# Graph network layer 0: the attention encoder as one run of steps, its exponentials traced two steps ahead across the parts, and the emptying of the PSUM banks queued behind them

## Chip, cores, metric

The kernel runs on one core of a Trainium2 chip. The metric is the device time of one launch in microseconds (us), the median of several launches. A profile is one further launch recorded by the hardware profiler. Engines are called by the names of the profile: PE is TensorE (matmul), PEld its weight load, DVE is VectorE, ACT is ScalarE, POOL is GpSimd, SP is SyncE, which here only issues DMAs.

## What is computed

Four graph layers follow each other on 2708 nodes with 512 features. Each is `x = layernorm(x + layer(x, adj))`. The change touches only the first attention of layer 0 (the "encoder"). The reference, cut to that part:

```python
n = X.shape[0]                                    # 2708 nodes, 512 features, H = 4 heads of D = 128
Xh = X.reshape(n, H, D).transpose(1, 0, 2)
Xw = jnp.einsum('hnd,hde->hne', Xh, W)
f1 = jnp.einsum('hnd,hd->hn', Xw, V[:, 0, :, 0])
f2 = jnp.einsum('hnd,hd->hn', Xw, V[:, 1, :, 0])
sig = jax.nn.sigmoid(f1[:, :, None] + f2[:, None, :])
...                                               # both patterns are adj, so local_att == long_att
att = softmax over the entries with adj != 0 of adj * sig
Xa = jnp.einsum('hij,hjd->hid', att, Xw)
Xc = Xa.transpose(1, 0, 2).reshape(n, F)
Xn = _batchnorm(Xc, enc_bn_gamma, enc_bn_beta)
emb = _mlp_block(Xn, enc_mlp_W, enc_mlp_b, enc_mlp_bn_gamma, enc_mlp_bn_beta)
...                                               # decoder: att applied to emb, then an MLP block
x = _layernorm(x + out)                           # layers 1 to 3 follow
```

## The kernel before

The softmax weights are never held as a whole. The target nodes (`i`) are split into two halves of 1354 (`hf`, `HSPAN`), the four heads into two pairs (`p`, `HP` = 2), and the source nodes (`j`) into `NT` = 22 blocks of up to 128. One of the four combinations (`hf`, `p`) is here called a **part**: (0,0), (0,1), (1,0), (1,1), in this order. A part walks over the 22 blocks in the order `ORDER`; a block of a part is a **step**, and its number in the part is `place`. So the encoder has 88 steps. `attention_pass` is called with `first=True` for the encoder, and again with `first=False` for the decoder.

`form` makes the weights of one step: a block of 128 sources by 1354 targets for two heads, in a tile `t` of 128 x 2708 floats. It loads a block `a` of the transposed adjacency (L378), and then

- in the parts with `p == 0` (`prepare`): turns zeros of `a` into a large negative number with two DVE instructions (`z` L394, `a` L395) and stores the block to DRAM as `adj_d` on the POOL queue (L399); parts with `p == 1` load that `adj_d` instead;
- two ACT instructions (L406): tanh of f1 + f2, one for each head, the tile `f1b` holding f1 spread over the partitions;
- one DVE instruction (L414) that adds a constant to tanh and multiplies by `a`;
- one ACT instruction (L415): the exponential, of both heads at once.

Some steps (`KEPT`) store `t` to DRAM as well (`kept`, L501, POOL queue), for the decoder. The wide tile `t` comes from a set of five buffers (`wide_tile`), the tile `a` from four, `f1b` from three.

`node_sums(k, ...)` (L436) then multiplies: for head `k` of the pair, 11 matmuls with 128 targets of `t` as weights and the 129 columns of `xw` (128 features and a column of ones for the sum of weights) as the moving operand. Both heads of a step are 2 x 22 records in the profile's count, 44 in all. All eight PSUM banks hold the sums of a part, four for each head, from its first step to its last.

At the end of a part `keep` is called (its result is named `turns`). It traces the **emptying** of the banks: for each head five groups, each of three DVE instructions (L643 clamp of the sum, L644 reciprocal, L645 multiplication into the tile `rows`, which also is one of the five wide tiles). It returns two functions `turn(0)` and `turn(1)`: each transposes the rows of one head on PE (L662, L670) into banks of head 1, copies them to `ft` on DVE (L672, L682), and leaves `bn_stats` (L684) in the list `later`. The loop of the next part calls them: at `place` 0 it traces head 0's sums and `turn(0)`, at `place` 1 head 0's sums and `turn(1)`; head 1's sums of these two steps wait in the list `waiting` until then, since the transposes use head 1's banks.

The order of work: the program traces instructions in the order of the Python code, and a planner at compile time orders each engine's queue by its own model of durations, the order of tracing being the priority; it also hands out the buffers and inserts the waits. Each engine runs its queue in that order. `tc.issue_after(ins)` adds an edge that puts the traced instructions of the same engine behind `ins`. In the kernel before, a dictionary `taken` holds the last L645 of each head; the `form` of `place` 2 of the next part is traced under `issue_after` of these, so that it comes behind the emptying.

Of the kernel before, what the change touches and what calls it, by code (L numbers as in the profile page):

```python
# [8 lines left out]
F32 = mybir.dt.float32  # L9
# [8 lines left out]
P = 128  # L18
# [11 lines left out]
def gnn_stack_kernel(  # L30
# [25 lines left out]
    nc = tc.nc  # L56
    N, F = x.shape
    H = w0.shape[1]
    C = F // P
    NT = (N + P - 1) // P  # L60
# [123 lines left out]
    with ExitStack() as l0:  # L184
# [143 lines left out]
        def spread_sums(att, hf, p):  # L328

            h0, w = HSPAN[hf]  # L330
            t = att.tile([P, HP, HW], F32, tag="rb", name="rb", bufs=1)
            for k in range(HP):
                nc.sync.dma_start(
                    t[:, k, :w], rs_d[HP * p + k, h0 : h0 + w].partition_broadcast(P)
                )
            return t
# [4 lines left out]
        def attention_pass(values, first, att, psum, finish, f1b=None, blocks=(), spread=None, rest=None, taken={}):  # L341
# [84 lines left out]
            def node_sums(k, place, jt, t, w, hf):  # L426

                n = BLOCKS[jt][1]
                slots = list(range(NB))
                if n < P:  # L430
                    slots.sort(key=lambda r: r % PER)
                for r in slots:
                    b, s = divmod(r, PER)
                    i0, m = NODES[hf][r]
                    own = 0 if n == P else b % HB * Q
                    nc.tensor.matmul(  # L436
                        po[k][b][:m, s * DR : (s + 1) * DR],
                        t[own : own + n, k, i0 : i0 + m],
                        values[own : own + n, jt, HP * pair + k, :],
                        start=(place == 0 and s == 0),  # L440
                        stop=(place == NT - 1),
                        skip_group_check=True,
                    )

            later = []
# [3 lines left out]
            turns = []  # L449
            for hf, (h0, w) in enumerate(HSPAN):  # L450
                for p in range(H // HP):
                    prepare = first and p == 0
                    if f1b is None or not prepare or hf > 0:
# [19 lines left out]
                    rb = None if first else spread_sums(att, hf, p)  # L473
                    pair = p
                    waiting = []
                    for place, jt in enumerate(ORDER):
                        n = BLOCKS[jt][1]


                        if place > (3 if first else 0) and later:  # L480
                            later.pop(0)()
                        if first:
                            t = wide_tile(att, "t")[:, : HP * HW].rearrange(
                                "p (k w) -> p k w", k=HP
                            )
                        else:
                            t = att.tile([P, HP, HW], F32, tag="t", name="t", bufs=4)
                        tv = t[:n, :, :w]
                        kept = kept_d.get((hf, p, jt))
                        if kept is None or first:  # L490
                            rows = n if n == P else HR
                            with ExitStack() as order:

                                for ins in taken.values() if place == 2 else ():
                                    order.enter_context(tc.issue_after(ins.ins))
                                step = form(hf, p, jt, att, prepare, f1b, t[:rows, :, :w])
                            if rest is not None:
                                rest(step)
                                rest = None
                            if kept is not None:  # L500
                                nc.gpsimd.dma_start(kept[:n, :, :w], tv)  # L501
                        else:
                            for r in range(0, P if n == P else HB * Q, P if n == P else Q):
                                nc.sync.dma_start(t[r : r + n, :, :w], kept[:n, :, :w])
                            if p == 0 and jt in KEPT[1]:
                                count(hf, jt, att)
                        if po is None:


                            both = [  # L510
                                psum.tile([P, HP, BANK], F32, tag=f"po{q}", name="po", bufs=1)
                                for q in range(HB)
                            ]
                            po = [both[q][:, k, :] for k in range(HP) for q in range(HB)]
                            if first:
                                more = [
                                    psum.tile([P, BANK], F32, tag=f"psm{k}", name="po", bufs=1)
                                    for k in range(HP)
                                ]
                                po = [  # L520
                                    [both[q][:, k, :] for q in range(HB)] + [more[k]]
                                    for k in range(HP)
                                ]
                        if first:
                            node_sums(0, place, jt, t, w, hf)
                            waiting.append(lambda a=(1, place, jt, t, w, hf): node_sums(*a))
                            if turns:
                                turns.pop(0)()
                            if not turns:
                                for work in waiting:  # L530
                                    work()
                                waiting = []
                            continue
                        for k in range(HP):
                            h = HP * p + k
                            for q, (q0, qw) in enumerate(HCH[hf]):
                                r = 0 if n == P else q * Q
                                nc.tensor.matmul(  # L538
                                    po[HB * k + q][:, :qw],
                                    values[r : r + n, jt, h * P : (h + 1) * P],  # L540
                                    t[r : r + n, k, q0 : q0 + qw],
                                    start=(place == 0),
                                    stop=(place == NT - 1),
                                )
                    if first:
                        turns = finish(hf, p, po, later)
                    else:
                        later += finish(hf, p, po, rb) or []
# [65 lines left out]
        with (  # L614
# [5 lines left out]
            taken = {}  # L620
            ft = feat_tile("ft")

            def keep(hf, p, po, later):
# [5 lines left out]
                for k in range(HP):  # L629
# [8 lines left out]
                    for b, g in groups:  # L638
# [6 lines left out]
                        taken[k] = nc.vector.tensor_tensor(  # L645
# [45 lines left out]
            attention_pass(xw, True, att, psum, keep, f1b, blocks, spread, rest, taken)  # L691
# [1378 lines left out]
```

## Time and profile before

| | us |
|---|---|
| median of 3 runs (lowest to highest) | 3199.09 (3196.76 to 3205.66) |
| the profiled execution: its own time | 3197.97 |
| the profiled execution: span from the first to the last instruction | 3196.2 |
| PE busy over the span | 3104.5 (97%) |
| DVE busy | 2050.9 (64%) |
| ACT busy | 1349.7 (42%) |
| encoder: first and last L436 matmul, about | 38.6 to 534.2 |

The mean granted TensorE clock is 0.989. A line of the timeline reads: start in us from the span's start, duration in us, engine, line of the kernel, operation, output and inputs with shapes, count, and in brackets the idle time of that engine just before, with what ended it. Runs of like instructions close together are merged in one line. A line of the windows view gives busy time and count for each engine in a stretch, then the granted clock, the share of DMA time and the transfer rate. A line of a group gives count, busy time and mean ns of one, and the idle time before it. A line of the waits view gives the total, the number and the longest of a kind of wait.

### The profile page before, as it was taken

Reading aid. Unit: us, or ns where it says so; the run is one execution under the profiler, and the core shown is the slowest. Engines: PE = TensorE matmul, PEld = TensorE weight load, DVE = VectorE, ACT = ScalarE, POOL = GpSimd, SP = SyncE. Lnnn points to the kernel's source line nnn. Section 1 sums busy time; section 2 is a strip of 40 time slices with the busy share of each in tenths; the row PEclk is TensorE's granted clock in tenths of the full one; section 3 lists DMA queues with packets and bytes.
Section 4 is the critical chain, followed back from the end, with each engine's and each line's share of the span. In section 5 each row is a group of like instructions: output and inputs, shape, how many; then the busy total and the mean of one; then the engine's idle time right before and its main releaser. Section 6 shows DMA issues by size and latency. Waiting matters only on the chain.

```text
span 3196.2 us, 39584 instructions
## 1 busy us (share of the span) xinstructions
PE 3104.5 (97%) x15176; PEld 2353.4 (74%) x15176; DVE 2050.9 (64%) x3797; ACT 1349.7 (42%) x1615; POOL 204.0 (6%) x304
## 2 busy tenths in 40 slices
PE   8998899999999999999999999999999999999999
PEld 7988887444444446885578787777668888888886
DVE  7878975777686684444167667767644555555565
ACT  7898887477867552001133333434301111111111
POOL 1100100000000000000011111110110000000000
PEclk9999999999999999999999999999999999999999
DMA  7866865146545413541144444556431111111111
GB/s 277 305 216 218 283 244 181 68 153 232 178 159 207 171 62 95 144 127 44 40 149 139 139 143 148 156 172 177 134 101 36 50 52 49 49 51 51 49 44 34
DMA packets 203635, 425.81 MB, mean 133 GB/s; under 512 B 20798, under 2 KB 134562, under 8 KB 197622
## 3 DMA queue, kind: packets, MB, share of 16 engines
q1 hardware_dynamic: 179454, 319.92, 32.3%
q0 software_dynamic: 23552, 101.26, 8.5%
q8 instruction: 119, 1.95, 0.2%
q10 hardware_dynamic: 440, 2.10, 0.2%
q14 instruction: 70, 0.57, 0.1%
HBM read 325.88 MB, written 95.87 MB: 132 GB/s over the span
## 4 chain that ended last, share of the span: by engine, by line
PE 76%; DVE 8%; issue 6%; ACT 5%; DMA 4%; POOL 1%; SPq 0%; DVEq 0%; POOLq 0%; ACTq 0%
PE po L1546 18%; PE ps_s L1342 17%; PE po L538 10%; PE ps_nb L1156 7%; PE po L436 6%; PE ps_wide L1206 5%; PE ps_sup L1734 2%; PE ps_mlp L792 2%; PE ps_hid L131 2%; ACT t L415 2%; ACT t L406 2%; PE ps_dec L923 2%; DVE t L414 2%; PE ps_v L131 1%; DVE e L1832 1%
## 5 line engine op out<-in xcount | busy, mean ns | idle before, releaser
L414 DVE SCALAR_TENSOR_TENSOR t<-t,a 128x2708 f32<-128x2708 f32 (+1 forms) x152 | 450.6, 2975 | 171.0 <-ACT t L406 165.4
L436 PE MATMUL po<-xw,t 128*128 128x129 f32 (+2 forms) x3872 | 444.2, 281 | 43.7 <-ACT t L415 42.6
L436 PEld LDWEIGHTS po<-xw,t 128*128 128x128 f32 (+2 forms) x3872 | 435.4, 192 | 52.0 <-ACT t L415 48.0
L406 ACT ACTIVATE t<-f1b,f2h 128x1354 f32<-128x1354 f32 (+1 forms) x304 | 414.3, 1412 | 55.0 <-PE po L538 33.2
L415 ACT ACTIVATE t<-t 128x2708 f32<-128x2708 f32 (+1 forms) x152 | 371.7, 2453 | 96.7 <-DVE t L414 96.3
L1342 PE MATMUL ps_s<-q,hT 128*128 128x256 f32 (+1 forms) x1848 | 405.5, 372 | 0.0
L538 PE MATMUL po<-t,emb 128*128 128x452 f32 (+3 forms) x1056 | 397.7, 545 | 3.9 <-ACT t L415 3.7
L1546 PE MATMUL po<-sup,e 128*128 128x256 f32 (+1 forms) x1512 | 397.0, 384 | 2.8 <-DVE c L1627 2.1
L1342 PEld LDWEIGHTS ps_s<-q,hT 128*128 128x128 f32 x1848 | 339.2, 190 | 49.8 <-issue 6.8
L538 PEld LDWEIGHTS po<-t,emb 128*128 128x128 f32 (+1 forms) x1056 | 193.6, 190 | 201.1 <-issue 190.6
L1546 PEld LDWEIGHTS po<-sup,e 128*128 128x128 f32 (+1 forms) x1512 | 264.3, 185 | 58.8 <-issue 21.5
L1546 PE MATMUL po<-held,T 128*128 128x256 f32 x1200 | 294.5, 380 | 4.5 <-DVE T L1503 4.5
L1546 PEld LDWEIGHTS po<-held,T 128*128 128x128 f32 x1200 | 226.4, 190 | 38.2 <-DVE T L1503 6.9
L1922 DVE SCALAR_TENSOR_TENSOR e<-a_cols,ps_s 128x512 f32<-128x512 f32 (+1 forms) x121 | 79.7, 659 | 239.4 <-PE ps_s L1342 233.3
L1342 PE MATMUL ps_s<-hT 128*128 128x256 f32 (+2 forms) x968 | 215.6, 374 | 4.1 <-DVE e L1832 2.5
L1342 PEld LDWEIGHTS ps_s<-hT 128*128 128x128 f32 x968 | 175.4, 191 | 31.9 <-DVE e L1832 2.9
L1828 ACT ACTIVATE a_score<-a_score,neg_big 128x512 f32<-128x512 f32 (+2 forms) x131 | 88.7, 686 | 250.1 <-DMA a_score<-in_adj_dram 102.8
L1156 PE MATMUL ps_nb<-hid_hi,at 128*128 128x512 f32 x484 | 185.5, 390 | 0.4 <-DVE at L1148 0.4
L1156 PE MATMUL ps_nb<-hid_lo,at 128*128 128x512 f32 x462 | 179.9, 389 | 0.0
L1452 ACT ACTIVATE e<-e 128x512 f32<-128x512 f32 (+1 forms) x187 | 113.5, 617 | 133.5 <-DVE e L1451 133.1
L1503 DVE TENSOR_TENSOR T<-e 128x256 f32<-128x256 f32 x200 | 83.9, 420 | 124.9 <-PE po L1546 99.2
L1914 ACT ACTIVATE q<-ps_wide,uq 128x256 f32<-128x256 f32 (+1 forms) x44 | 20.5, 465 | 338.4 <-PE ps_wide L1206 338.4
(275 smaller groups left out, 3938.6 us busy)
## 6 DMA issues: line engine op xcount, KB each, us to landing
a<-adj_d SPq DMA_DIRECT2D x108, 677.0 KB
a_cols<-in_adjT_dram SPq DMA_DIRECT2D x200, 256.0 KB
a<-in_adjT_dram SPq DMA_DIRECT2D x42, 677.0 KB
adj_d<-a POOLq DMA_DIRECT2D x42, 677.0 KB, 6.0
kept<-t POOLq DMA_DIRECT2D x20, 1354.0 KB, 7.6
t<-kept SPq DMA_DIRECT2D x20, 1354.0 KB
raw<-in_adjT_dram SPq DMA_DIRECT2D x105, 256.0 KB
a_score<-in_adjT_dram SPq DMA_DIRECT2D x55, 256.0 KB
```

Source lines behind the costliest of these rows:

```text
L131: nc.tensor.matmul(ps[:n], xt[:, c, :n], w[:, c, :], start=(c == 0), stop=(c == C - 1))
L406: tanh = nc.scalar.activation(tv[:, k, :], f1b[k][:n, :w], AF.Tanh, bias=f2h[:n, jt, h : h + 1], scale=0.5,)
L414: step = nc.vector.scalar_tensor_tensor(tv, tv, GUARD, ab, ALU.add, ALU.mult)
L415: exp = nc.scalar.activation(tv, tv, AF.Exp, scale=0.5)
L436: nc.tensor.matmul(po[k][b][:m, s * DR : (s + 1) * DR], t[own : own + n, k, i0 : i0 + m], values[own : own + n, jt, HP * pair + k, :], sta ...
L538: nc.tensor.matmul(po[HB * k + q][:, :qw], values[r : r + n, jt, h * P : (h + 1) * P], t[r : r + n, k, q0 : q0 + qw], start=(place == 0), ...
L1156: nc.tensor.matmul(pos[it][:n], at, half[:, jt, :], start=(jt == 0 and k == 0), stop=(jt == NT - 1),)
L1206: nc.tensor.matmul(ps[:, :width], w(c, o), xt(c), start=(c == 0), stop=(c == C - 1),)
L1342: nc.tensor.matmul(ps[:, jb, i:w], keys[:, c, j : j + P], st["q"][:, c, i:], start=(c == 0), stop=(c == C - 1),)
L1452: nc.scalar.activation(e, e, AF.Exp)
L1546: nc.tensor.matmul(po[bank][rows, half, :], lhsT, rhs, start=(k == 0 and half == 0) if first is None else first, stop=last, skip_group_che ...
L1828: nc.scalar.activation(a, a, AF.Identity, bias=neg_big[: a.shape[0]], scale=1.0e30)
```

## The change

The nested loops over halves, pairs and blocks become one loop over a list `steps` of 88 (for the encoder) with an index `k`. In the encoder, `front` = 2: iteration `k` traces the `form` of step `k`, and then the sums (`node_sums`) of step `k - 2`, whose tile waits in the list `held`. So when the last sums of a part are traced, the first two steps of the next part have been formed already; their `f1b` loads are traced two steps earlier as well. The emptying (`finish`, which is `keep`) is traced under `issue_after(last_step)`, `last_step` being the L414 of the latest formed step, and each `turn` likewise. `taken` and its edges are gone. `later` is looked at beside the sums rather than before `form`. The sums of the decoder move into `feature_sums`, with `front` = 0; the order in which the decoder is traced stays. In `keep` nothing else changes. The core of the diff:

```diff
-        def attention_pass(values, first, att, psum, finish, f1b=None, blocks=(), spread=None, rest=None, taken={}):
+        def attention_pass(values, first, att, psum, finish, f1b=None, blocks=(), spread=None, rest=None):
...
-            def node_sums(k, place, jt, t, w, hf):
+            def node_sums(k, part, place, t):
+                hf, p = part
+                jt = ORDER[place]
...
-            turns = []
-            for hf, (h0, w) in enumerate(HSPAN):
-                for p in range(H // HP):
+            turns, waiting, held = [], [], []
+            parts = [(hf, p) for hf in range(NHALF) for p in range(H // HP)]
+            steps = [(part, place) for part in parts for place in range(NT)]
+            front = 2 if first else 0
+            last_step, rb = None, None
+            for k in range(len(steps) + front):
+                if k < len(steps):
+                    (hf, p), place = steps[k]
+                    h0, w = HSPAN[hf]
+                    jt = ORDER[place]
+                    n = BLOCKS[jt][1]
                     prepare = first and p == 0
-                    if f1b is None or not prepare or hf > 0:
+                    if place == 0 and (f1b is None or k > 0):
...
-                            with ExitStack() as order:
-                                for ins in taken.values() if place == 2 else ():
-                                    order.enter_context(tc.issue_after(ins.ins))
-                                step = form(hf, p, jt, att, prepare, f1b, t[:rows, :, :w])
+                        last_step = form(hf, p, jt, att, prepare, f1b, t[:rows, :, :w])
+                        if rest is not None:
+                            rest(last_step)
+                            rest = None
+                        if kept is not None:
+                            nc.gpsimd.dma_start(kept[:n, :, :w], tv)
...
-                        if first:
-                            node_sums(0, place, jt, t, w, hf)
-                            waiting.append(lambda a=(1, place, jt, t, w, hf): node_sums(*a))
-                            if turns:
-                                turns.pop(0)()
-                            if not turns:
-                                for work in waiting:
-                                    work()
-                                waiting = []
-                            continue
...
-                    if first:
-                        turns = finish(hf, p, po, later)
+                    held.append(t)
+                if k < front:
+                    continue
+                part, place = steps[k - front]
+                t = held.pop(0)
+                if po is None:
+                    po = banks()
+                if not first:
+                    feature_sums(part, place, t)
+                    if place == NT - 1:
+                        later += finish(*part, po, rb) or []
+                    continue
+                if place > 3 and later:
+                    later.pop(0)()
+                node_sums(0, part, place, t)
+                waiting.append(lambda a=(1, part, place, t): node_sums(*a))
+                if turns:
+                    with tc.issue_after(last_step.ins):
+                        turns.pop(0)()
+                if not turns:
+                    for work in waiting:
+                        work()
+                    waiting = []
+                if place == NT - 1:
+                    with tc.issue_after(last_step.ins):
+                        turns = finish(*part, po, later)
...
             def keep(hf, p, po, later):
-                        taken[k] = nc.vector.tensor_tensor(
+                        nc.vector.tensor_tensor(
```

## Prediction

> **What bounds the kernel now.** I read the page first: PE is busy 97% of the span, so only time in which PE stands or runs slowly can be won. The change touches the encoder alone, so next the windows view, cut at the three crossings from one part to the next.
>
> ```profile
> core 0: us, PE busy (x) PEld busy (x) DVE busy (x) ACT busy (x) POOL busy (x), PEclk, DMA share, GB/s
> 38.00:155.00 117.00, 106.73 (x916) 103.63 (x909) 111.30 (x68) 102.33 (x61) 17.62 (x31) 0.96 0.81 283
> 155.00:183.00 28.00, 20.41 (x156) 20.01 (x156) 21.90 (x44) 20.84 (x14) 2.01 (x4) 0.82 0.58 194
> 183.00:275.00 92.00, 91.40 (x839) 90.77 (x838) 59.68 (x29) 90.27 (x55) 5.34 (x11) 1.00 0.68 233
> 275.00:301.00 26.00, 18.08 (x138) 17.61 (x137) 20.85 (x44) 17.84 (x12) 2.12 (x3) 0.80 0.55 206
> 408.00:434.00 26.00, 18.37 (x139) 17.84 (x138) 19.96 (x40) 20.38 (x13) 1.55 (x3) 0.80 0.64 225
> ```
>
> Part (0,0), the row from 38 to 155, is bound by DVE (111.3 of 117 us); part (1,0) alike. Part (0,1), 183 to 275, has PE and ACT full together and DVE at 60. At each crossing nobody is full, and the granted clock falls to 0.8. In the last part 918 matmuls of L436 took 101.05 us on the chain, 0.110 us each; at that price the 433 PE records of the three crossings need 47.7 us, and the crossings last 80. So 32 us is the ceiling of what the change can win.
>
> Then the timeline of the first crossing:
>
> ```profile
> 149.79 2.98 DVE L414 SCALAR_TENSOR_TENSOR t<-t,a 128x2708 f32<-128x2708 f32 x1
> 152.81 2.46 ACT L415 ACTIVATE t<-t 128x2708 f32<-128x2708 f32 x1 [3.03 <-DVE t L414]
> 155.18 7.98 ACT L406 ACTIVATE t<-f1b,f2h 128x1354 f32<-128x1354 f32 x6
> 159.49 0.16 DVE L643 TENSOR_SCALAR rc<-po 128x1 f32<-128x1 f32 x1 [6.72 <-PE po L436]
> 163.99 2.97 DVE L414 SCALAR_TENSOR_TENSOR t<-t,a 128x2708 f32<-128x2708 f32 x1
> 166.99 2.46 ACT L415 ACTIVATE t<-t 128x2708 f32<-128x2708 f32 x1 [3.83 <-DVE t L414]
> 169.50 5.10 PE L436 MATMUL po<-xw,t 128*128 128x129 f32 x22 [7.59 <-ACT t L415]
> 176.33 2.69 PE L436 MATMUL po<-xw,t 128*128 128x129 f32 x22
> 180.78 1.27 DVE L682 COPY ft<-po 128x512 f32<-128x512 f32 x2
> ```
>
> DVE finishes the part's last block at 152.8, idles 6.72 us for the last sums, and empties most of the banks; only then, at 163.99, does it multiply the next part's first block. Its exponential ends at 169.4, and PE, done at 161.9, waits 7.59 us, though head 0's banks were empty long before. Then its 22 matmuls take 5.10 us instead of 2.69. The second crossing:
>
> ```profile
> 260.76 0.87 DVE L394 TENSOR_SCALAR z<-a 128x1354 f32<-128x1354 f32 x1 [4.82 <-DMA a<-in_adjT_dram]
> 274.18 5.35 ACT L406 ACTIVATE t<-f1b,f2h 128x1354 f32<-128x1354 f32 x4
> 279.64 0.16 DVE L643 TENSOR_SCALAR rc<-po 128x1 f32<-128x1 f32 x1 [5.48 <-PE po L436]
> 289.65 5.10 PE L436 MATMUL po<-xw,t 128*128 128x129 f32 x22 [7.59 <-ACT t L415]
> ```
>
> The waits view of the encoder gives both waits in total:
>
> ```profile
> PE po L436 <- ACT t L415: 42.6, 20, 7.6
> DVE rc L643 <- PE po L436: 23.5, 4, 6.7
> ```
>
> **The change part by part.** No arithmetic is added or removed. What moves is the order of three queues around three crossings. Call the next part's steps n0, n1, n2, n3.
>
> *Crossings one and three (from p = 0 to p = 1).* In p = 0 ACT's tanh already runs two steps ahead of its exponentials (the part's last tanh is at 141.87, the last exponential at 152.81), so I expect n0's and n1's tanh in ACT's gaps before 157. Three things must be there. `f1b` was issued at 139.65; the first one of the kernel, issued at 22.9, held its tanh until 30.5, so 7.6 us, 147.3. The block `a`: SP issued at 141.5 and later, landing 5.2 to 11.5 us after, 153 at worst for n0. A wide tile: that of the step five earlier, done on PE at 142. Then on DVE n0 runs 152.8 to 155.8 and n1 to 158.8 (2 x 2.98), inside the 6.72 us of idling: cost nothing, covered by that idle time; without it, 5.95 us of delay of the emptying. The emptying starts at 159.5 as before and, without the multiplications between, lasts 6.2 us (4.6 from 159.49 to 164.1, and 1.6 for the pieces that stood behind L414), until 165.7; head 0's half is done by 162.6. PE: n0 of head 0 162.6 to 165.0 (22 x 0.11); transposes of `turn(0)` once head 1's banks are empty, 165.7 to 167.2; n1 to 169.7; transposes of `turn(1)` to 171.1.
>
> Now the new edges. The copies of each `turn` go behind L414 of n2 and n3: n2 165.7 to 168.7, copies 2.0 us to 170.7, n3 to 173.7, copies to 175.7. What is queued behind them: head 1's sums of n0 wait for banks that `turn(1)` uses. Before, these copies ended at 182.5 (rows 180.78 to 182.46), with n3 already ahead of them, so the edge adds nothing to that order. Head 1 starts at 175.5 instead of 182.5, with the same work behind it on PE: 7.0 us. If n1's tanh stays behind the exponential at 152.81, n1's L414 ends at 160.9 and everything is 1.4 later: 5.6 us. I take 7.0, by the steady order. Part (0,1) must keep the gain: it is full on ACT, 9.95 us for two steps in the timeline (4 tanh, 2 exponentials), and ACT's exponential of n3 moves from 181.6 to about 173.8, 7.8 us, so ACT does not eat it.
>
> *Crossing two (from p = 1 to p = 0).* Here DVE bounds what follows, so its finish counts. Before, both L414 and the emptying are done at 291.3. ACT is full; it makes n0's and n1's tanh at 274.18. If they stay there, n0's L414 ends at 279.8, n1's at 282.8, the emptying at 289.0: 2.3 us. With n0's tanh one exponential earlier (PE has three steps in hand at 267, so the displaced exponential is not late) L414 ends at 277.2 and 281.3, the emptying at 287.5: 3.8. Ceiling 5.5, the whole idle time. I take 3.5.
>
> *What else moves.* SP's loads of `f1b` and `a` and POOL's stores keep their order among themselves; `kept` of n1 is issued some ten us earlier, in crossings whose DMA share is 0.55 to 0.64. The six bn_stats after a crossing (0.67 each at most) move about two steps: in p = 1 DVE has 4.09 idle us in two steps, in p = 0 they cost the same as before. The `front` = 0 pass is traced in the old order: nothing. The last part's end has nothing to be formed ahead: nothing. The removed edge of `taken` lets n2 pass the emptying; its tile comes free only at about 157, so its L414 is ready near 163, behind most of it: zero taken, at worst 3 us at each crossing.
>
> *The clock.* Trace: after 7.59 idle us, 22 matmuls took 5.10; the same 22 at 176.33, after 11 transposes and short waits, 2.69. The Trainium skill (TensorE: Matmul & The Clock Gate, Part 1) has PE fall to half rate after an idle window of about 3.4 us, and its Part 4 says that transposes do not count as busy. By the trace, waits of 0.7 us with transposes between keep the full rate, which is what I summed. By Part 4 the stretch 165 to 171, transposes and waits for half of it, could still fall to half; then 22 matmuls cost 2.4 more at each of the two crossings that count, and the sum is 12.7. The row at 176.33 decides for the first.
>
> **Sum.** 7.0 + 3.5 + 7.0 = 17.5 us off the profiled execution's 3198.0: 3180.5. The median of the runs stands 1.1 above it: 3181.6, I say 3182. A difference of 0.3%, 9.6 us, is about what a measurement of this kernel can tell from no change.
>
> **The rivals.**
>
> *Half of it (chance 0.18).* n2 passes the emptying, or n0 and n1 get no tanh in time: the emptying starts 3 us late at each crossing. 17.5 - 9 = 8.5 us, or 10 where the slip is 2.5: 3189 to 3191. For: DVE takes its queue in order, as at 260.76, where a block that needs no load stood behind one that waited 4.82 us. Against: loads and tiles are early in the rows above.
>
> *It does not do what it says (0.09).* The planner keeps the old order on ACT (tanh after the last exponential, as at 155.18) and hides nothing: 0 to 5 us, 3194 to 3199. Against: the new edge forces L414 of n1 ahead of the emptying.
>
> *Slower (0.08): wide tiles.* Two formed tiles are held beside `rows` and the two in use, all five. If in the steady part a tanh then waits for a tile, the price falls on every step. Place: L406 waiting for PE L436. At 0.35 us in each of 88 steps it costs 31, net +13: 3212. It decides from 17.5 / 88 = 0.2 us a step. Against: tanh waits only 2.5 us for PE L436 in all the encoder now, and tiles come free by PE's pace, which the tracing order does not change.
>
> *More than the sum (0.05).* The second crossing fills its whole 5.5, and ACT's 7.8 decides at the others with no leftover wait: beyond 28 us, under 3171, needs nearly the ceiling of 32.
>
> **How the numbers follow.** The main case has 0.60 and spans 3172 to 3189 (each crossing up to 2.5 us worse or 3 better). Faster by over 9.6 us: 0.60 + 0.05 + 0.11 of the half case: 0.76. Within: 0.07 + 0.09 = 0.16. Slower: 0.08. The range 3169 to 3194 leaves out the slower case, part of the unchanged one and the far end of the gain, some 0.17.
>
> **What would show it.** Right: two L414 between the part's last and the first L643 at each crossing; PE's wait ahead of L436 there under 3 us instead of 7.59; 22 matmuls in about 2.5 us; granted clock of the crossings above 0.9; the last L436 near 517 instead of 534. Wrong: L643 waiting for L414 well after PE is done; tanh waiting for PE L436 in the middle of parts; the encoder's end unmoved, or moved while a later stage gives it back.

## The result, and the profile after

| | before | the change |
|---|---|---|
| median of the runs | 3198.95 us (8 runs) | 3190.35 us (8 runs) |
| lowest to highest | 3196.30 to 3205.66 | 3185.02 to 3196.62 |
| ratio, 95% interval | | 0.9973 [0.9962, 0.9984] |
| profiled execution: span | 3196.2 us | 3194.8 us |
| of it, encoder (start of the first L414 to the start of the last matmul of the sums) | 502.0 us | 497.2 us |

The change is 8.6 us faster. The time lies inside the range of the prediction (3169 to 3194), but outside its main case (3172 to 3189), and the gain is half of the forecast 17.5 us. The profiled execution of the change happens to be its longest run (3196.62 us), so the spans of the two profiles show next to none of the gain. Below, gains and losses *inside* the encoder are read from the profiles, and what a version is *worth* is read from the ratios. The need for this shows in the stretch after the encoder: its code is the same in most versions, and in the profiles it took between 2657.1 and 2667.4 us.

The windows view of the change, cut at the same three crossings as before:

```profile
core 0: us, PE busy (x) PEld busy (x) DVE busy (x) ACT busy (x) POOL busy (x), PEclk, DMA share, GB/s
155.00:183.00 28.00, 21.33 (x174) 20.62 (x173) 23.47 (x49) 20.66 (x13) 3.08 (x6) 0.94 0.68 224
275.00:301.00 26.00, 16.97 (x130) 16.77 (x129) 22.55 (x46) 17.37 (x11) 1.55 (x3) 0.80 0.55 196
408.00:434.00 26.00, 21.04 (x158) 20.57 (x159) 20.25 (x48) 17.76 (x11) 2.55 (x5) 0.87 0.68 233
```

The granted clock rose at crossings one and three, from 0.82 to 0.94 and from 0.80 to 0.87, and stayed at 0.80 at crossing two. PE's busy time in the three rows together went from 56.9 to 59.3 us: 2.5 us more in windows of 80. The crossings are hardly fuller than they were. The waits view of the encoder says what took the place of the old wait:

```profile
PE po L438 <- ACT t L415: 25.7, 15, 5.0
PE po L438 <- DVE rows L658: 13.4, 5, 9.0
```

(Total us, number, longest.) PE's wait for the exponential fell from 42.6 us to 25.7; 13.4 us of waiting for the emptying of the banks stand beside it now, 9.0 of them in one piece. The timeline of the first crossing shows the first part of the reason:

```profile
147.84 0.86 DVE L394 TENSOR_SCALAR z<-a 128x1354 f32<-128x1354 f32 x1
151.01 2.98 DVE L414 SCALAR_TENSOR_TENSOR t<-t,a 128x2708 f32<-128x2708 f32 x1 [2.31 <-DMA a<-adj_d]
153.91 1.56 DVE L395 SCALAR_TENSOR_TENSOR a<-z,a 128x1354 f32<-128x1354 f32 x1
155.50 5.87 DVE L414 SCALAR_TENSOR_TENSOR t<-t,a 128x2708 f32<-128x2708 f32 x2
161.03 7.63 PE L438 MATMUL po<-xw,t 128*128 128x129 f32 x52 [4.47 <-ACT t L415]
165.36 0.16 DVE L656 TENSOR_SCALAR rc<-po 128x1 f32<-128x1 f32 x1 [3.97 <-PE po L438]
169.86 2.97 DVE L414 SCALAR_TENSOR_TENSOR t<-t,a 128x2708 f32<-128x2708 f32 x1
173.35 0.94 PE L438 MATMUL po<-xw,t 128*128 128x129 f32 x6 [1.68 <-DVE rows L658]
```

The multiplication at 151.01 reads a block of `adj_d`: it belongs to the *next* part (n0), for only p = 1 reads `adj_d`. It stands between the two preparing instructions (L394 and L395) of the old part's last block. So the last block waits for 2.31 us of a load that it does not need and for 2.98 us of a multiplication that nobody needs yet. Its own L414, first of the pair at 155.50, ends at 158.4; before, it ended at 152.8. PE stands for 4.47 us *before* the last sums, and the emptying starts at 165.36 instead of 159.49. The last two lines show a smaller cost: n2's multiplication, at 169.86, stands ahead of the last pieces of the emptying, and PE then waits 1.68 us for these. The second crossing:

```profile
272.18 5.35 ACT L406 ACTIVATE t<-f1b,f2h 128x1354 f32<-128x1354 f32 x4
277.34 0.87 DVE L394 TENSOR_SCALAR z<-a 128x1354 f32<-128x1354 f32 x1 [3.58 <-DMA a<-in_adjT_dram]
279.72 5.86 DVE L414 SCALAR_TENSOR_TENSOR t<-t,a 128x2708 f32<-128x2708 f32 x2
285.51 0.15 DVE L656 TENSOR_SCALAR rc<-po 128x1 f32<-128x1 f32 x1
288.54 2.92 PE L438 MATMUL po<-xw,t 128*128 128x129 f32 x12 [9.03 <-DVE rows L658]
```

The tanh of n0 is done by 274.9 (two of the four from 272.18). Yet L414 of n0 and n1 start at 279.72, because the preparation of n3, two steps after n1, stands ahead of them and waits 3.58 us for its load. PE finished the old part at 279.51 (288.54 less 9.03) and then idled 9.03 us.

Set side by side, the order in which VectorE gets its work is this, in the change and in a version with two more edges (`e3_both`, below). "Last" is the old part's last block; n0 to n3 are the next part's steps; z and a are L394 and L395. n2's multiplication, which stands inside the emptying in both, is left out.

```
crossing one   change:   z(last)  L414(n0)  a(last)  L414(last)  L414(n1)  emptying
               e3_both:  z(last)  a(last)   L414(last)  L414(n0)  L414(n1)  emptying
crossing two   change:   z,a(n2)  z,a(n3)   L414(n0)  L414(n1)  emptying
               e3_both:  z,a(n2)  L414(n0)  L414(n1)  emptying, with z,a(n3) inside it
```

The prediction had assumed the order of `e3_both`.

### The profile page after: what moved, and what is told of

It reads as the page before. It is cut to its first block, busy times and chain, and to the rows that moved or that the text cites. A ratio compares the mean times of both kernels' runs of the same rounds, so it can differ in the third digit from the quotient of the medians.

```text
span 3194.8 us, 39584 instructions
## 1 busy us (share of the span) xinstructions
PE 3106.3 (97%) x15176; PEld 2354.7 (74%) x15176; DVE 2052.8 (64%) x3797; ACT 1349.8 (42%) x1615; POOL 206.5 (6%) x304
## 4 chain that ended last, share of the span: by engine, by line
PE 74%; DVE 8%; issue 7%; ACT 5%; DMA 4%; POOL 1%; SPq 0%; DVEq 0%; POOLq 0%; ACTq 0%
PE po L1559 18%; PE ps_s L1355 17%; PE po L456 10%; PE ps_nb L1169 7%; PE ps_wide L1219 5%; PE po L438 4%; PE ps_hid L131 2%; PE ps_sup L1747 2%; PE ps_mlp L805 2%; ACT t L406 2%; ACT t L415 2%; PE ps_dec L936 2%; DVE t L414 2%; PE ps_v L131 1%; DVE e L1845 1%
## 5 line engine op out<-in xcount | busy, mean ns | idle before, releaser
L414 DVE SCALAR_TENSOR_TENSOR t<-t,a 128x2708 f32<-128x2708 f32 (+1 forms) x152 | 450.3, 2975 | 175.0 <-ACT t L406 164.8
L438 PE MATMUL po<-xw,t 128*128 128x129 f32 (+2 forms) x3872 | 445.1, 282 | 39.9 <-ACT t L415 25.7
```

The lines of the kernel that those rows point to most:

```text
L414: step = nc.vector.scalar_tensor_tensor(tv, tv, GUARD, ab, ALU.add, ALU.mult)
L438: nc.tensor.matmul(po[k][b][:m, s * DR : (s + 1) * DR], t[own : own + n, k, i0 : i0 + m], values[own : own + n, jt, HP * p + k, :], start= ...
```

## The experiments

The theory (A): forming ahead is worth what was predicted, about 17.5 us, but the order on VectorE takes half of it back: n0 ahead of the last block at crossings one and three, the preparation of n3 ahead of n0 at crossing two. Rivals: the new `issue_after` edges of the emptying hold something; the gain is bounded by another thing (tiles, loads, ACT), so that the order does not matter; the loop form or the removed `taken` edges, not the forming ahead, made the difference. The versions were timed in three series (e1 to e4, e5 to e8, e9 to e12), each with the kernel before among them. "Encoder" below is its length in the one profiled execution of each version.

| version | median us (before in the same series) | ratio, 95% interval | encoder us |
|---|---|---|---|
| e1_old_first | 3182.76 (3201.75) | 0.9936 [0.9922, 0.9951] | 488.5 |
| e2_z_late | 3191.39 (3201.75) | 0.9962 [0.9949, 0.9974] | 494.0 |
| e3_both | 3181.22 (3201.75) | 0.9931 [0.9919, 0.9944] | 483.1 |
| e4_no_edges | 3191.65 (3201.75) | 0.9961 [0.9949, 0.9974] | 496.5 |
| e5_change_again | 3191.85 (3200.53) | 0.9970 [0.9957, 0.9983] | 491.6 |
| e6_front1 | 3200.02 (3200.53) | 0.9994 [0.9986, 1.0002] | 502.6 |
| e7_five_a | 3193.19 (3200.53) | 0.9976 [0.9968, 0.9984] | 496.8 |
| e8_front0 | 3200.56 (3200.53) | 0.9998 [0.9990, 1.0007] | 499.7 |
| e9_tanh_late | 3187.84 (3200.34) | 0.9960 [0.9947, 0.9972] | 489.4 |
| e10_both_again | 3180.16 (3200.34) | 0.9944 [0.9930, 0.9957] | 484.6 |
| e11_old_first_again | 3184.23 (3200.34) | 0.9953 [0.9941, 0.9965] | 486.7 |
| e12_front3 | 3202.76 (3200.34) | 1.0004 [0.9996, 1.0012] | 503.8 |

**e1_old_first: the old part's last block first.** One edge at each crossing: L414 of n0 goes behind the old part's last L414. (`and True` is a switch between e1, e2 and e3.)

```diff
-                step = nc.vector.scalar_tensor_tensor(tv, tv, GUARD, ab, ALU.add, ALU.mult)
+                with tc.issue_after(behind.ins) if behind else nullcontext():
+                    step = nc.vector.scalar_tensor_tensor(tv, tv, GUARD, ab, ALU.add, ALU.mult)
...
+                        behind = last_step if first and k > 0 and place == 0 and True else None
```

> One edge is added to the changed kernel: at each crossing, L414 of the next part's first block (n0) is queued behind L414 of the old part's last block. In the changed kernel VectorE has n0 ahead of the last block at crossings one and three, and waits 2.31 us there for n0's load. Theory A (the order is what failed): without that, the last block is ready 2.31 + 2.98 = 5.3 us earlier, the emptying starts at about 160 instead of 165.4, head 1's sums follow some 4 us earlier at each of crossings one and three, and the encoder ends 8 us earlier: about 3182 us. Rival B (only the late load costs): the order does not matter, the wait for the load goes, 2.3 us at each of two crossings: about 3186 us. Rival C (ScalarE or a later stage takes back whatever the crossings give): 3190 us, with the emptying earlier but the last L438 matmul where it is now.

Measured: 0.9936, 19 us under before (16 us in the repetition, e11), where the change had 8.6. The emptying starts at 162.79, 281.57 and 407.48, against 165.36, 285.51 and 415.89 in the change. PE's longest idle times at crossings one and three are 1.68 and 1.61 us instead of 4.47 and 5.03; crossing two keeps 7.74. One edge, which adds no work and takes none away, about doubles the gain: the order at crossings one and three cost about what had been missing.

**e2_z_late: the preparation of n3 later.** The other edge alone, at crossing two: z of n3 goes behind L414 of n1.

```diff
-                    nc.vector.tensor_scalar(z[:n, :w], a[:n, :w], 0.0, None, ALU.is_equal)
+                    with tc.issue_after(zbehind.ins) if zbehind else nullcontext():
+                        nc.vector.tensor_scalar(z[:n, :w], a[:n, :w], 0.0, None, ALU.is_equal)
...
+                        zbehind = steps_done[-2] if first and hf > 0 and prepare and place == 3 and True else None
```

> One edge is added to the changed kernel: in the part (1,0) the two instructions that prepare block n3 (z, a) come behind L414 of n1. In the changed kernel they stand ahead of L414 of n0, and VectorE waits 3.58 us for n3's load at crossing two, with the emptying behind. Theory A: L414 of n0 starts when its tanh is done, about 275 instead of 279.7, the emptying at about 281 instead of 285.5, PE's wait of 9.0 us falls to about 5, and since VectorE bounds the part that follows, the encoder ends 2.5 to 3.5 us earlier: about 3187 us. Rival C: PE waits less at crossing two and the encoder's end stays: 3190 us.

Measured: 0.9962. L414 of n0 and n1 run from 275.66 instead of 279.72, the emptying starts at 281.46 instead of 285.51, and PE's idle time there falls from 9.03 to 6.56 us. So the edge does its work at the place. The wait that it removes is not the same in every execution: 3.58 us in the first profile of the change, 2.32 in the second (e5), 2.29 in e1. Its worth in the total is not resolved: the interval overlaps those of the change ([0.9962, 0.9984] and, in e5, [0.9957, 0.9983]).

**e3_both, and e10_both_again:** both edges.

> Both edges together. Theory A: the two gains add, 8 + 3 us: about 3179 us, which is the forecast of the change as such (3182) reached by an order that I had assumed. Rival B: 4.6 + 0 us, 3186. Rival C: 3190.

> The kernel of e3 again, beside e11, to size the second edge (block n3 prepared behind n1 at crossing two). Expected as in e3: 0.993 of the kernel before, an encoder of 481 to 487 us, 2.5 to 3.5 us shorter than e11.

Measured: 0.9931 and 0.9944, about 20 us under before in both series; the encoder is 18.9 and 17.4 us shorter than the 502.0 of before. This version beats both kernels. Timeline of crossings one and two of `e3_both` (L416 is the multiplication here, L417 the exponential, L440 the sums, L662 to L664 the emptying):

```profile
150.74 8.76 DVE L416 SCALAR_TENSOR_TENSOR t<-t,a 128x2708 f32<-128x2708 f32 x3
158.49 5.17 PE L440 MATMUL po<-xw,t 128*128 128x129 f32 x44 [1.21 <-ACT t L417]
161.24 0.16 DVE L662 TENSOR_SCALAR rc<-po 128x1 f32<-128x1 f32 x1 [1.74 <-PE po L440]
164.28 1.99 PE L440 MATMUL po<-xw,t 128*128 128x129 f32 x14 [0.62 <-DVE rows L664]
...
270.88 5.87 DVE L416 SCALAR_TENSOR_TENSOR t<-t,a 128x2708 f32<-128x2708 f32 x2 [0.96 <-ACT t L407]
276.68 0.15 DVE L662 TENSOR_SCALAR rc<-po 128x1 f32<-128x1 f32 x1
282.02 4.57 PE L440 MATMUL po<-xw,t 128*128 128x129 f32 x20 [6.56 <-DVE rc L662]
```

The three multiplications stand in one run (last, n0, n1), VectorE idles 1.74 us where it idled 6.72, and PE goes from the old part to the new at crossing one with waits of at most 1.61 us. At crossing two it still waits 6.56. The windows view of `e3_both` at the three crossings:

```profile
155.00:183.00 28.00, 24.56 (x215) 23.71 (x214) 25.59 (x50) 24.90 (x16) 2.55 (x5) 1.00 0.59 213
275.00:301.00 26.00, 19.44 (x157) 19.23 (x156) 25.50 (x51) 20.80 (x14) 3.59 (x6) 0.87 0.51 183
408.00:434.00 26.00, 24.39 (x220) 24.14 (x219) 22.99 (x26) 22.89 (x15) 2.56 (x5) 1.00 0.58 196
```

PE is busy for 68.4 us of 80 now (before 56.9, the change 59.3), at full clock at crossings one and three.

**e11_old_first_again:** e1 once more, beside e10, to see whether the second edge is worth anything on top of the first.

> The kernel of e1 again: 0.9936 to 0.994 of the kernel before, an encoder of 485 to 490 us. If it is as short as e10, the second edge is worth nothing that can be told.

Measured: 0.9953 [0.9941, 0.9965] beside 0.9944 [0.9930, 0.9957]; in the first series 0.9936 beside 0.9931. Both series put the version with the second edge ahead, by 1.5 and 4.1 us in the medians (5.4 and 2.2 in the encoders), and both times the intervals overlap. Its size stays open.

**e4_no_edges:** the two `issue_after(last_step.ins)` around `finish` and `turns` taken away.

```diff
-                    with tc.issue_after(last_step.ins):
-                        turns.pop(0)()
+                    turns.pop(0)()
...
-                    with tc.issue_after(last_step.ins):
-                        turns = finish(*part, po, later)
+                    turns = finish(*part, po, later)
```

> The changed kernel without its new edges: the emptying and the two turns are not queued behind L414; only the tracing two steps ahead is left. If the tracing order alone sets VectorE's queue (theory D), n0 and n1 stay ahead of the emptying, and the time is that of the changed kernel, 3190 within 3 us. If the edges carry the change (rival E), the emptying goes ahead of n0 and n1 again and the time is that of the kernel before, 3199.

Measured: 0.9961, with the change's order on VectorE: n0's L414 ahead of the last block (after a wait of 3.73 us for its tanh), the emptying from 166.33, 284.88 and 415.23. The edges that the change's description names do nothing that the order of tracing does not do already. They neither bring the gain nor hold it back.

**e5_change_again:** the change, not altered, in the second series.

> The changed kernel once more, beside the next three on one chip, and to see how far the length of its encoder (first L414 to last L438 matmul, 497.2 us in its first profile, 502.0 in the kernel before) moves from execution to execution. Expected: 0.997 of the kernel before, an encoder of 496 to 499 us, and the same order on VectorE with the two waits for loads, each within 2 us of what it was.

Measured: 0.9970 [0.9957, 0.9983], as the first time. Its encoder was 491.6 us long where 496 to 499 was expected: a miss, and the measure of how far one profile of an encoder can be trusted, some 3 us to either side of the mean of the two. n0's L414 waited at the same place, this time 3.58 us for its tanh rather than 2.31 us for its load.

**e6_front1 and e8_front0:** fewer steps ahead. `front` is 1 in e6; in e8 it is 0, with the edges of e4 taken away as well, so that only the loop form and the removed `taken` are left of the change.

> The changed kernel with one step traced ahead instead of two (edges kept). VectorE then has only n0 ahead of the last block at crossings one and three, and n1 behind the emptying. Theory A: n0 still costs the old part its 3 us and the wait for the load, but the emptying starts 3 us earlier than with two ahead; n1 comes after it, in time for TensorE, which has head 0 of n0 and the transposes to do: the encoder is as long as with two ahead, within 3 us, 494 to 500 us, about 3190 us in all. Rival F (two ahead is what fills the crossing): one ahead gives half of the gain, an encoder of 499 to 501 us, about 3195 us.

> The changed kernel with nothing traced ahead and without the new edges: what is left against the kernel before is one loop instead of three and the missing edge behind the emptying. Theory D (tracing ahead carries the change): the kernel before, an encoder of 501 to 503 us, 3199 us, the emptying ahead of n0 at each crossing. Rival G (the removed edge carries it): an encoder under 499 us.

Measured: 0.9994 and 0.9998, both no different from before. So the loop form is worth nothing, nor are the removed edges of `taken` as long as nothing is formed ahead; what the change brings comes from the steps formed ahead. With two steps ahead the edges were not put back: there n2's multiplication stands ahead of the emptying's last pieces, and whether an edge behind these would win PE's 1.68 us is not shown. But one step ahead should have brought part of it (an encoder of 494 to 500 us was expected; it took 502.6). Two lines of its timeline show what stood in the way:

```profile
151.32 2.98 DVE L414 SCALAR_TENSOR_TENSOR t<-t,a 128x2708 f32<-128x2708 f32 x1 [2.31 <-DMA a<-adj_d]
283.91 0.87 DVE L394 TENSOR_SCALAR z<-a 128x1354 f32<-128x1354 f32 x1 [5.07 <-DMA a<-in_adjT_dram]
```

n0 stands ahead of the last block here too, with the same wait, and at crossing two a preparation waits 5.07 us ahead of n0. The cost of the order is paid, for half of what is formed ahead. The emptying starts no earlier for having n1 behind it (166.48, against 165.36 in the change; 3 us earlier was expected), since it waits there for the old part's last sums, which PE began at 161.34, and not for n1. One step ahead with the order mended was not run.

**e7_five_a:** is it the late load, rather than the place in the queue? A fifth buffer for the blocks `a`, paid for by z in bf16; two weight blocks loaded behind the encoder move from z's buffer to those of `a` (not shown in the cut). The order stays that of the change.

```diff
-                    a = att.tile([P, HW], F32, tag="a", name="a", bufs=4 if first else 3)
+                    a = att.tile([P, HW], F32, tag="a", name="a", bufs=5 if first else 3)
...
-                    z = att.tile([P, HW], F32, tag="z", name="z", bufs=1)
+                    z = att.tile([P, HW], BF16, tag="z", name="z", bufs=1)
```

> The changed kernel with five buffers for the blocks of the adjacency instead of four; to make room the mask z is held as bfloat16 (its values are 0 and 1). The order on VectorE at crossings one and three stays: n0 ahead of the last block. The loads are issued a step earlier, so the wait for n0's load (2.31 us in the changed kernel) should go. Theory A (order): that alone gives 2.3 us at each of the two crossings, and n0's 2.98 us still stand ahead of the last block: an encoder of 491 to 494 us, longer than the 488.5 with the order mended. Rival B (late load alone): as good as the mended order, 489 us or less. A shorter z instruction, if bfloat16 makes it one, shortens the parts with p = 0 besides; that is to be read from its own row.

Measured: 0.9976; the encoder took 496.8 us, above the 491 to 494 expected by the one and well above the 489 of the other theory. The first crossing, and the second:

```profile
152.63 2.98 DVE L414 SCALAR_TENSOR_TENSOR t<-t,a 128x2708 f32<-128x2708 f32 x1 [4.20 <-ACT t L406]
278.98 0.87 DVE L394 TENSOR_SCALAR z<-a 128x1354 bf16<-128x1354 f32 x1 [5.25 <-DMA a<-in_adjT_dram]
```

At crossing one the load of n0 is in time, and its L414 waits 4.20 us for its tanh instead; the emptying starts at 165.41, as in the change. (At crossing two the load of n3 is late even with the fifth buffer, by 5.25 us, so there the version does not separate load from order.) It is not one late input: a step that stands ahead of an urgent one waits for whichever of its inputs comes last.

**e9_tanh_late:** if ACT gives the old part's last exponential before n1's tanh, do the last sums come earlier? On top of e3, the tanh of n1 goes behind the exponential of the old part's last block (in parts with p = 1).

```diff
-                turn = opening.get(jt) if prepare and hf == 0 else None
+                turn = opening.get(jt) if prepare and hf == 0 else tbehind
...
-                        last_step = form(hf, p, jt, att, prepare, f1b, t[:rows, :, :w], behind, zbehind)
+                        last_step = form(hf, p, jt, att, prepare, f1b, t[:rows, :, :w], behind, zbehind, exps[-2] if first and p == 1 and place == 1 else None)
```

> Both edges of e3, and one more at crossings one and three: ScalarE makes the tanh of n1 only behind the exponential of the old part's last block. In e3 that exponential stood behind n1's tanh, which waited 2.27 us for a tile still being stored, and TensorE waited 1.21 us for it. Theory A carried to ScalarE: TensorE finishes the old part some 2 us earlier, but n1's L414 is then 1 to 2 us later and holds the emptying: 0 to 2 us gained at each of two crossings, an encoder of 479 to 483 us, a ratio of 0.992 to 0.993. Rival: n1 is late and holds the emptying by as much as was won: the time of e3.

Measured: 0.9960 and an encoder of 489.4 us, worse than expected under either theory: 7.7 us behind e10 in the medians of the same series, though the intervals overlap. (The multiplication is L416 here, the sums L441.)

```profile
160.84 2.98 DVE L416 SCALAR_TENSOR_TENSOR t<-t,a 128x2708 f32<-128x2708 f32 x1 [4.62 <-PE po L441]
167.12 5.07 PE L441 MATMUL po<-xw,t 128*128 128x129 f32 x22 [5.19 <-DVE rows L666]
```

The last sums do come earlier: PE ends the old part at 161.93 instead of 163.66. But n1's multiplication now starts only at 160.84, when its tanh is done, and stands ahead of the emptying, which is needed first and starts at 163.75 instead of 161.24; PE idles 5.19 us, and its next 22 matmuls take 5.07.

**e12_front3:** three steps ahead, on top of e3.

> Both edges of e3 with three steps traced ahead instead of two. The third block n2 has its L414 ahead of the emptying too. Theory A: DVE's idle time at crossings one and three (5.3 to 6.7 us before the change) holds two L414 of 2.98 us, not three; the third delays the emptying by 3 us, but it need not be done after it: no gain over e3, an encoder of 482 to 486 us. Rival H (the more ahead the better): under 480 us. Rival I (wide tiles run out: three formed, the rows and two in use are six, and there are five): tanh waits for PE at the crossings, over 488 us.

Measured: 1.0004 and an encoder of 503.8 us. The gain is gone, where 482 to 486 us had been expected. (Lines as in `e3_both`.)

```profile
165.60 2.98 DVE L416 SCALAR_TENSOR_TENSOR t<-t,a 128x2708 f32<-128x2708 f32 x1 [6.52 <-ACT t L407]
171.88 4.46 PE L440 MATMUL po<-xw,t 128*128 128x129 f32 x22 [8.41 <-DVE rows L664]
```

By the trace it is again an instruction put ahead of an urgent one (no edge was run to test it): n2's multiplication, at 165.60, stands ahead of the emptying (168.50 here) and waits 6.52 us for its tanh, and PE idles 8.41, 12.82 and 8.96 us at the three crossings. The timeline of ACT shows why the tanh is late: ACT is busy without a gap from 155.8, and the second tanh of n2 comes at 164.16, behind the exponentials of n0 and n1. That the five wide tiles run out, the reason given in rival I, whose figure of over 488 us came true, is not what the waits show: in all the encoder, tanh waits 4.6 us for PE's sums here, and 4.6 in e3.

## Why the prediction was right in part

Gains against before at three points of the timeline, in us (positive is earlier), each from one profile of one execution:

| | prediction | e3_both | e10_both_again | e1_old_first | the change |
|---|---|---|---|---|---|
| PE ends part (0,1), before: 282.06 | 7.0 | 6.6 | 8.1 | 5.2 | 2.6 |
| emptying starts at crossing three, before: 412.53 | 10.5 | 10.1 | 9.6 | 5.1 | -3.4 |
| last matmul of the encoder's sums starts, before: 534.0 | 17.5 | 18.0 | 17.6 | 13.0 | 4.2 |

**The sum was right for the order that it assumed.** In e3 and e10 the three crossings bring 7.0 + 3.5 + 7.0 within about 2 us at every point. So the 7.0 us of crossing one and "ACT does not eat it" for part (0,1) (the gain of crossing one arrives at its end, 6.6 and 8.1) are borne out. Of the 3.5 of crossing two, 3.5 and 1.5 came, and there PE's side was not as forecast: the signs named for a right prediction, a wait under 3 us and a clock above 0.9, hold in e3 at crossings one and three (waits up to 1.61, clock 1.00) but not at two (6.56 and 0.87). The last L436 near 517 became 516 in both.

**That the time fell inside the range was luck.** The main case ended at 3189; what reached as far as 3190.35 was the share of the half case, and the mechanism of that case is not what happened.

**The step that failed** is "Then on DVE n0 runs 152.8 to 155.8 and n1 to 158.8, inside the 6.72 us of idling: cost nothing". In the change n0 does not run behind the last block but ahead of it, from 151.01, after a wait. The cost is 5.6 us of delay of the last block (158.4 against 152.8): 2.31 of waiting, 2.98 of multiplication, and a small rest between the two profiles. The emptying starts 5.9 us late, and of the 7.0 us at crossing one 2.6 are left. (The copies of `turn(1)` end at 182.66 in the kernel before and at 175.7 in the sum, where the prediction has 182.5 and 175.5; the 7.0 stays.) The bounds given for n0's inputs held (the load "153 at worst", it came near 151.0; the tanh before 157), that of the load by luck: the 5.2 to 11.5 us are the landings of POOL's stores of `adj_d` (issued at 138.90, 144.46 and 149.96), and the trace has none for SP's loads. But they bounded when n0 *could* run, and n0 came earlier in the queue than its inputs came. I had not asked what that does to the block behind it: the cover named, idle time *after* the last block, is no cover for work put *ahead* of it.

**The second term mis-sized is crossing two's 3.5.** With n3's preparation ahead of n0, its wait and its two instructions (3.58 + 0.87 + 1.57 us, of which L414 of n0 loses 4.8, from 274.9 to 279.7) the emptying starts at 285.51, 6 us after PE was done with the part. This is the mark that the prediction named as wrong: "L643 waiting for L414 well after PE is done". Crossing three then repeats crossing one: its emptying is 3.4 us late, its end 4.2 early.

**The rivals.** *Half of it* had the time (8.5 us forecast, 8.6 measured) and the place (the emptying late at each crossing) but not the mechanism: n2 passed only the last pieces of the emptying (PE's 1.68 us at 173.35), long after its late start, and n0 and n1 had their tanh ahead of the old order. What came true is the reason given for it, that VectorE takes its queue in order; the word against it, that loads are early, was beside the point. *It does not do what it says* is refuted: PE's waits for the exponential fell by 17 us. *Wide tiles*: tanh waits 7.2 us in all for PE's sums in the change, 2.5 before, and 4.6 in e3; the mechanism is there, but a small part of the 31 us that the rival needs. *More than the sum* is refuted even for the best version.

**Costed at nothing, and so it was:** the loop form (e8) and the new edges (e4). `taken` was worth nothing with nothing formed ahead (e8); behind two formed steps, where "at worst 3 us" was said, it was not put back.

**The clock.** The lower sum of 12.7, from the statement in the Trainium skill (TensorE: Matmul & The Clock Gate, Part 4) that transposes do not count as busy in the same way, did not come true: in e3 the stretch from 164.3 to 174.8 is transposes, short sums and waits up to 1.61 us, and the window's clock is 1.00. A stretch of transposes alone did not occur. But the row at 176.33, by which the prediction decided, does not show that the rate is *kept*: in the kernel before the clock was 0.50 from 165.3 to 175.5 us and 1.00 after that, so the row begins 0.8 us after the return.

The idle window of about 3.4 us after which PE falls to half rate, in the Trainium skill (TensorE: Matmul & The Clock Gate, Part 1), holds here in one direction. After 5.19 us of idling PE did 22 matmuls in 5.07 us (e9), twice the time of full rate, and in the 14 traces each of the 43 idle times of 3.19 us or more inside the encoder was followed by a lowered clock within 3.4 us. Shorter ones went both ways: after 1.68 us PE did 88 matmuls in 10.15 us (e1, 0.115 each), at full rate. In the kernel before, 3.14 us at 384.99 were followed by the full rate, and 2.37 us at 360.38 by the half:

```profile
384.99 29.96 PE L436 MATMUL po<-xw,t 128*128 128x129 f32 x264 [3.14 <-ACT t L415]
359.80:363.20 3.40, 2.82 (x13) 2.83 (x14) 3.20 (x3) 2.68 (x3) 0.54 (x1) 0.51 0.95 368
```

(The first is a line of the timeline, 0.113 us a matmul; the second one of the windows view, clock 0.51.) So a sum that lets PE idle for less than 3.4 us cannot count on the full rate.

**What stays open.** Why the planner puts n0 ahead of the last block is not shown; no run looked into its costs and due times. At crossing two PE still idles 6.56 us in e3, while n3's preparation (0.86 + 1.55 us from 276.76) runs inside the emptying; a version with it behind the emptying was not tried.

## What to carry to other kernels

When work is formed ahead to fill an idle time, ask where it enters the queue of each engine, not only whether it fits into the idle time: an instruction that is ahead of an urgent one delays it by its duration *and* by its wait for its own latest input. If a planner orders the queues, look up the order that it made before believing the sum, and pin the one or two places that matter with an edge; here two edges at the crossings, without any change of the work, turned 9 us into 20. How far ahead to form has to be tried too: three steps lost the gain of two; by the trace, the third multiplication stood ahead of the emptying and waited there for its tanh. One step brought nothing, but was run only with the order not mended.

## What the runs showed of the hardware

- z written in bf16 instead of f32 (128x1354, from f32) took VectorE 0.86 us as before (859 against 858 ns mean): the narrower output brought no speed.
- The same program's encoder differed by 5.6 us between two profiled executions (497.2 and 491.6) while the medians of the runs agreed within 1.5 us (3190.35 and 3191.85). A single profile tells where time lies, not what 5 us are worth.
